# Block 1 loaded in two transfers, a root from ScalarE, LoRA four at a time, and a token sum in two parts: the start of a gated feed-forward kernel

## The chip, the cores and the metric

One core of a Trainium2 chip runs the program. A core has TensorE (PE; its weight loads are shown as PEld), VectorE (DVE), ScalarE (ACT), GpSimd (POOL) and SyncE (SP), which issues most of the DMAs. The metric is the device time of one execution in microseconds (us); before the change it is 442.54 us, the median of 3 runs (442.51 to 442.62).

## The reference

The input x is 2 x 1024 x 512 in f32, so 2048 tokens of 512 values.

```
xn = (x - mean) / sqrt(var + 1e-5)                  # over the 512 values of a token
s  = convolution of xn[token] with a kernel K of length 512, + D * xn
h1 = xn @ w1.T + 2 * (xn @ A1.T) @ B1.T             # 512 -> 1376, LoRA of rank 16
h3 = xn @ w3.T + 2 * (xn @ A3.T) @ B3.T
f  = (silu(h1) * h3) @ w2.T + 2 * (... @ A2.T) @ B2.T
out = x + s * silu(f)
```

The kernel merges each LoRA product into the weight it belongs to. K comes from the parameters of a state-space model; that part lies late in the program and the change doesn't touch it.

## The kernel before, in words

All matmuls are in f32, and TensorE makes two passes of each. The products with w1 and w3 use a fast matrix multiplication of Winograd's kind at two levels: seven products in place of eight, twice. Its operands are sums of quarters of the tokens and of the weights. They are called here T1 to T4 (sums of tokens) and sums of weights; "outer" sums are of the first level and "inner" ones of the second. VectorE makes nearly all of them.

**Tokens.** They stand in four blocks of 512, each of four tiles of 128 tokens. For a block, `load_x` (L225) requests the tiles, `norm_stats` (L244) takes mean and variance of each on VectorE (L247, L248), `norm_root` (L278) makes 1/sqrt(var + eps) by an integer guess and two corrections (`rsqrt`, L50, eight steps, behind one that adds eps and ahead of one that makes the shift), `normalize` (L288) applies it, tiles 0 and 2 on ScalarE (L293) and tiles 1 and 3 on GpSimd (L297), and `transpose` (L299) turns a tile by TensorE (four matmuls with the identity, L304) into a bank of PSUM, from which ScalarE copies it into `xr` (L312, or L314 and L315 for odd blocks). Blocks 0 and 1 make the first pair (sb 0), 2 and 3 the second. Block 3's statistics are made by ScalarE (L254, L265), and one `norm_root` serves blocks 2 and 3. `outer_token_sum` (L317, operations at L328) makes T1 to T4 of a pair in `xt`; `inner_token_sum` (L335) makes the inner sums, T3 at L341, T2 = T3 + b11 at L343, T4 at L345, T1 at L347, each in a raw part over the three rows of `xr` and a second part over the four rows of `xt`. Their results lie in `t_in[7]`, `t_in[6]` and `t_in[4]`; the last two are also where blocks 3 and 2 are loaded.

**Weights.** The hidden 1376 columns are five pairs of 2 x 128 and a last chunk of 96. `load_pair` (L396) fetches a pair's w1 and w3 in four transfers, `load_last` (L463) the last chunk in two. A LoRA product (`lora_product`, L381, matmul at L383) has a contraction of only 16 rows; the factors lie in four groups of 16 rows, at partitions 0, 32, 64 and 96: `lo_d` holds A1 or A3, `lo_h` a part of B1 or B3. Groups 0 and 2 hold the w1 factors, 1 and 3 the w3 factors. `merge_pair` (L408) uses groups 0 and 1 and does one half of a pair; `merge_whole_pair` (L419) uses all four groups for a whole pair at once. The products go into PSUM banks and VectorE adds them to the weights (`merge`, L392, operation at L393).

**Banks.** PSUM has eight banks, two each of the tags x, y, w and aux; `bank(tag)` takes them in turn, and with `borrow` it takes the next one without moving the turn.

**Order.** Each engine runs its instructions in the order in which the program records them, and the order is written out by hand: `at(place, what)` puts a step into a heap, and the heap is emptied in order of place (49 units of place are one pair's seven chains). `after(delay, what)` places a step behind the one now running. A `Chain` (L766 and on) is one product of the second level in seven steps, whose matmuls are all at L756, with copies by ScalarE at L776 and L794 and totals by VectorE at L780. The code ahead of the heap (L965 to L1020) is recorded first, in order: loads, 36 passes on the identity that keep TensorE busy (`keep_warm`), the last chunk's LoRA product, block 0's statistics, root and normalization, four more keep-warm matmuls, block 0's transposes, and then block 1's statistics and root with the merges of the last chunk (L484) between them. The last chunk's product with the first token pair (`last_chain`) is the first real product.

**DMA.** SP and ACT have a queue each. Eight DMA semaphores go round over all transfers of both: a transfer waits, on the engine that issues it, until the eighth before it has landed.

In the built program the first transfers stand so on the two queues:

```
SP : x tiles 0, 2 | lo_d, lo_h group 0 | block 1, four tiles | last w1, w3 | pair 0 (4) |
     blocks 2, 3 (8 tiles) | pair 1 (4) | lo_d, lo_h group 2 | lo_d, lo_h group 3
ACT: x tiles 1, 3 | lo_d, lo_h group 1 | table load
```

Of the kernel before, what the change touches and what calls it, by code (L numbers as in the profile page):

```python
# [12 lines left out]
F32 = mybir.dt.float32  # L13
I32 = mybir.dt.int32
AF = mybir.ActivationFunctionType
# [34 lines left out]
def rsqrt(nc, pool, v, shape):  # L50


    y = pool.tile(shape, F32, tag="rs_y", name="rs_y")
    t = pool.tile(shape, F32, tag="rs_t", name="rs_t")
    part = 3.0 / 8.0
    c2 = part * 0.703952253
    nc.vector.tensor_scalar(
        y.bitcast(I32), v.bitcast(I32), -0.5, float(0x5F1FFFF9), ALU.mult, ALU.add
    )
    nc.vector.tensor_tensor(t, y, y, ALU.mult)  # L60
    nc.vector.scalar_tensor_tensor(t, t, -c2, v, ALU.mult, ALU.mult)
    nc.vector.scalar_tensor_tensor(y, t, c2 * 2.38924456, y, ALU.add, ALU.mult)
    nc.vector.tensor_tensor(t, y, y, ALU.mult)
    nc.vector.scalar_tensor_tensor(t, t, 1.0 / part**2, v, ALU.mult, ALU.mult)
    nc.vector.scalar_tensor_tensor(t, t, -10.0 / 3.0, t, ALU.add, ALU.mult)
    nc.vector.scalar_tensor_tensor(y, t, 5.0, y, ALU.add, ALU.mult)
    return y
# [40 lines left out]
def s4_gated_ffn(  # L108
# [59 lines left out]
    def bank(tag, borrow=False):  # L168

        i = turn[tag]  # L170
        if not borrow:
            turn[tag] = 1 - i
        return psum.tile([P, 512], F32, tag=f"{tag}{i}", name=tag, bufs=1)
# [36 lines left out]
    def value(tag="s"):  # L210
        return upool.tile([P, TB], F32, tag=tag, name=tag, bufs={"s": 10, "c": 4}[tag])
# [7 lines left out]
    def after(delay, what):  # L219
        at(now[0] + delay, what)  # L220
# [2 lines left out]


    def load_x(b):  # L225
        room = (None, None, t_in[4], t_in[6])[b]
        tiles = []
        for tt in range(NTT):
            t = value() if room is None else room[:, tt, :]
            queue = nc.scalar if b == 0 and tt % 2 else nc.sync  # L230
            queue.dma_start(out=t, in_=x[bass.ds(b * TB + tt * P, P), :])
            tiles.append(t)
        return tiles

    norms, sums_of_x = {}, {}

# [38 lines left out]
            norms[b][:, :, 1], sums_of_x[b][:, 2, :], 1.0 / DIM, None, mult  # L275
        )

    def norm_root(mv, *blocks):  # L278
        n = len(blocks) * NTT
        veps = small.tile([P, n], F32, tag="veps", name="veps")  # L280
        nc.vector.tensor_scalar(veps, mv[:, :, 1], EPS, None, add)
        rstd = rsqrt(nc, small, veps, [P, n])
        shift = small.tile([P, n], F32, tag="shift", name="shift")
        nc.vector.scalar_tensor_tensor(shift, mv[:, :, 0], -1.0, rstd, mult, mult)
        for n, b in enumerate(blocks):
            norms[b] = [t[:, n * NTT : (n + 1) * NTT] for t in (rstd, shift)]
# [9 lines left out]
            else:  # L296
                nc.gpsimd.tensor_scalar(t, t, rstd[:, one], shift[:, one], mult, add)  # L297

    def transpose(b, tiles, tag="aux"):  # L299
        sb, low = divmod(b, 2)  # L300
        for tt in tiles:
            ps = bank(tag)
            for dc in range(NDC):
                nc.tensor.transpose(  # L304
                    ps[:, dc * P : (dc + 1) * P],
                    x_in[b][tt][:, dc * P : (dc + 1) * P],
                    ident,
                )
            at_ = slice(tt * P, (tt + 1) * P)
            halves = ps.rearrange("p (c k t) -> p c k t", c=2, k=2)  # L310
            if low == 0:
                nc.scalar.copy(xr[:, 0:2, sb, :, at_], halves)  # L312
            else:
                nc.scalar.copy(b12[sb][:, :, at_], halves[:, 0])  # L314
                nc.scalar.copy(xr[:, 2, sb, :, at_], halves[:, 1])  # L315
# [18 lines left out]

    def inner_token_sum(name, raw, half=None):  # L335
        src, lo, n = (xr, 0, 3) if raw else (xt, 3, 4)
        some = slice(n) if half is None else slice(2 * half, 2 * half + 2)
        to = {i: t[:, lo : lo + n, :][:, some] for i, t in t_in.items()}
        b11, b21, b12_, b22 = (src[:, some, s, k, :] for s in range(2) for k in range(2))
        if name == 3:  # L340
            nc.vector.tensor_tensor(to[7], b22, b12_, sub)  # L341
        elif name == 2:
            nc.vector.tensor_tensor(to[6], to[7], b11, add)  # L343
        elif name == 4:
            nc.vector.tensor_tensor(to[4], b21, to[6], sub)  # L345
        else:
            nc.vector.tensor_tensor(b12_, b12_, b11, sub)  # L347
# [21 lines left out]
    def load_lora(queue, group, d, h, lo, hi):  # L369
        rows = slice(32 * group, 32 * group + R)  # L370
        if d is not None:
            queue.dma_start(out=lora["d"][rows, :], in_=d)
        queue.dma_start(out=lora["h"][rows, : hi - lo], in_=h[:, lo:hi])
        lora["base"][group] = lo
# [6 lines left out]
    def lora_product(ps, group, dc, lo, n, start=True):  # L381
        d, h = lora_factors(group, lo, n)
        nc.tensor.matmul(  # L383
            ps,
            lhsT=d[:, dc * P : (dc + 1) * P],
            rhs=h,
            start=start,
            stop=True,
            skip_group_check=True,
        )  # L390

    def merge(to, ps):  # L392
        nc.vector.scalar_tensor_tensor(to, ps, LORA_SCALE, to, mult, add)  # L393
# [11 lines left out]
                )  # L405
        return w

    def merge_pair(c, w, half, tag="aux"):  # L408

        ps = [bank(tag), bank(tag)]  # L410
        for k in range(2):
            for v in range(2):
                n = slice(k * 2 * P, (k + 1) * 2 * P)
                lora_product(ps[v][:, n], v, 2 * half + k, PAIR_AT[c], 2 * P, k == 0)
        for v in range(2):
            to = w[:, (1, 2, 0, 3)[2 * v + half]].rearrange("p k m h -> p (k m h)")
            after(1.6 + v, lambda to=to, v=v: merge(to, ps[v]))

    def merge_whole_pair(c, w, first=None, delays=(1.15, 2.3, 4.3, 4.4)):  # L419

        ps = [first or [bank("y", True), bank("w", True)], [bank("aux"), bank("aux")]]
# [41 lines left out]
    def load_last():  # L463
        both = const.tile([P, 2, 2 * NDC * LASTR], F32, tag="w2b", name="last")
        w, s = (
            both[:, i].rearrange("p (a b h) -> p a b h", a=n, h=LASTR)
            for i, n in enumerate((2, 4))
        )
        for v, src in enumerate((w1T, w3T)):
            nc.sync.dma_start(  # L470
                out=w[:, v], in_=src[:, LAST * P :].rearrange("(dc p) h -> p dc h", p=P)
            )
        return w, s

    def lora_last():
        ps = [bank("y"), bank("y")]
# [485 lines left out]
        for i, p in places:  # L962
            at(7 * n + p, lambda i=i: step(i))

    x_in = {0: load_x(0)}  # L965
    warm = const.tile([P, 1], F32, name="warm")
    nc.gpsimd.memset(warm, 0.0)
    make_identity(nc, ident)
    lora_tiles(LSPLIT)
    factors = (a1, b1T), (a3, b3T)  # L970
    for v, f in enumerate(factors):
        load_lora((nc.sync, nc.scalar)[v], v, *f, LSPLIT, HID)
    nc.scalar.activation(warm, warm, AF.Silu)
    x_in[1] = load_x(1)
    make_upper_triangular(nc, tri, 1.0, diag=True)
    w_last, s_last = load_last()
    w_pair, s_pair = {0: load_pair(0)}, {c: {} for c in range(NPAIR)}
    x_in[2], x_in[3] = load_x(2), load_x(3)
    w_pair[1] = load_pair(1)
    for v, f in enumerate(factors):  # L980
        load_lora(nc.sync, 2 + v, *f, LSPLIT, HID)

    def other_factors():
        for v, (_, h) in enumerate(factors):
# [18 lines left out]
    ps_last = lora_last()  # L1003
    mv = norm_tile(0)
    norm_stats(0, range(NTT))
    norm_root(mv, 0)
    normalize(0)

    keep_warm(primed[1], 4)
    transpose(0, range(NTT))  # L1010
    mv = norm_tile(1)
    norm_stats(1, range(2))
    merge_last(w_last, ps_last, 0)
    norm_stats(1, range(2, NTT))
    norm_root(mv, 1)
    merge_last(w_last, ps_last, 1)
    mv_late = norm_tile(2, 3)
    ab_last = last_operands(w_last, s_last)

# [37 lines left out]
            add_chain(2 + 7 * c + n, pair_chain(c, n), places)  # L1057
    at(-10, lambda: normalize(1))
    at(-9.9, lambda: last_sums(w_last, s_last))
    at(-9, lambda: merge_pair(0, w_pair[0], 0))  # L1060
    at(-3.8, lambda: merge_pair(0, w_pair[0], 1))
    for i in range(2):
        at(-6 + i, lambda i=i: transpose(1, range(2 * i, 2 * i + 2), "y"))
    for n, name in enumerate((3, 2, 1)):
        at((-2.3, -1.5, -0.45)[n], lambda name=name: outer_token_sum(0, name))
        at(-0.6 + 0.3 * n, lambda name=name: outer_weight_sums(w_pair[0], (name,)))
    at(0.4, lambda: outer_token_sum(0, 4))
    at(0.8, lambda: outer_weight_sums(w_pair[0], (4,)))
    for tt in range(NTT):
        at(-6 + 0.8 * tt, lambda tt=tt: norm_stats(2, (tt,)))  # L1070
        at(-1.4 + 0.1 * tt, lambda tt=tt: act_sums(3, tt))
        at((-0.3, -0.2, 1.7, 1.8)[tt], lambda tt=tt: act_squares(3, tt))
    at(-0.9, lambda: act_means(3))
    at(1.9, lambda: act_variances(3))
    at(6.9, lambda: norm_root(mv_late, 2, 3))
    at(7.3, lambda: normalize(2))
    at(7.7, lambda: normalize(3, (0,)))
    for n, place in enumerate((12.1, 12.8, 13.7, 14.4)):
        b, i = divmod(n, 2)
        at(place, lambda b=b, i=i: transpose(2 + b, range(2 * i, 2 * i + 2)))  # L1080
# [5 lines left out]
        at(when, lambda name=name: inner_weight_sum(w_pair[0], s_pair[0], name))  # L1086
    for name, raw, when, *half in (
        (3, True, 21.6),
        (2, True, 22.8),
        (3, False, 24.2),  # L1090
        (2, False, 30.2),
        (1, True, 34.4),
        (1, False, 37.5, 0),
        (1, False, 40.3, 1),
        (4, True, 47.6),
        (4, False, 50.2, 0),
        (4, False, 52.3, 1),
    ):
        at(when, lambda of=(name, raw, *half): inner_token_sum(*of))
# [495 lines left out]
```

## Time and profile before

| | us |
|---|---|
| median of 3 runs | 442.54 |
| the profiled execution | 442.84 |
| its span, first to last instruction | 441.0 |
| TensorE busy | 434.3 (98%) |
| VectorE busy | 317.6 (72%) |
| GpSimd busy | 207.9 (47%) |
| ScalarE busy | 144.3 (33%) |
| DMA, mean | 122 GB/s |

The page shows one execution. Busy time of TensorE is modelled: its matmuls overlap, and a matmul that waits a little still looks busy, so the distance from one start to the next is the better measure (0.43 us for a pass over 512 columns, 0.11 us over 128). The chain of waits follows the execution back from its end and tells at each step what released it. A timeline merges neighbours of one kind; "x8" behind a row says how many, and the bracket behind it how long the engine was idle and for whom. Times in timelines count from the start of the span.

### The profile page before, as it was taken

What the parts mean: (1) busy time and instruction counts of PE and PEld (TensorE: products, weight loads), DVE (VectorE), ACT (ScalarE), POOL (GpSimd) and SP (SyncE); (2) the same over time, 40 slices, a digit from 0 to 9 for tenths busy, and PEclk for the clock granted to TensorE, in tenths of its full rate; (3) what the DMA queues carried; (4) which work ended last, traced back from release to release, by engine and by line L of the source; (5) the groups of instructions that cost most, each with busy time, mean ns of one, the idle gap of its engine ahead of it and who ended that gap; (6) DMA issues with size and microseconds to landing.
All of it is one profiled execution on the core that took longest, in us unless ns stands there. A gap on an engine that the chain in (4) does not pass through costs nothing.

```text
span 441.0 us, 5158 instructions
## 1 busy us (share of the span) xinstructions
PE 434.3 (98%) x1704; PEld 269.1 (61%) x1704; DVE 317.6 (72%) x536; ACT 144.3 (33%) x296; POOL 207.9 (47%) x156
## 2 busy tenths in 40 slices
PE   7999999999999999999999999999999999999996
PEld 7645334344444444444443446888898999999996
DVE  5899999954974687469745796979786885653234
ACT  2777242453255324532453242211101212212221
POOL 1416468895689368946894468400000122222221
PEclk9999999999999999999999999999999999999999
DMA  8931304025102500250035526395901832422211
GB/s 242 364 83 44 124 0 149 10 84 159 36 24 80 159 24 25 88 170 25 25 129 206 162 94 214 94 364 189 344 33 71 296 129 95 144 97 95 77 67 48
DMA packets 35467, 53.61 MB, mean 122 GB/s; under 512 B 4689, under 2 KB 21521, under 8 KB 35313
## 3 DMA queue, kind: packets, MB, share of 16 engines
q1 hardware_dynamic: 35088, 52.69, 36.3%
q10 hardware_dynamic: 352, 0.60, 0.4%
q8 instruction: 13, 0.21, 0.2%
q14 instruction: 14, 0.11, 0.1%
HBM read 33.88 MB, written 19.40 MB: 121 GB/s over the span
## 4 chain that ended last, share of the span: by engine, by line
PE 86%; DVE 7%; DMA 2%; ACT 2%; issue 1%; POOL 0%; SPq 0%; DVEq 0%; ACTq 0%; POOLq 0%
PE x L756 43%; PE y L756 22%; PE w L756 11%; PE aux L930 4%; PE w L930 2%; DMA s<-in_x_dram 1%; DVE xt L328 1%; DVE s L453 1%; DVE w L441 1%; DMA w<-in_w1T_dram 1%; PE y L529 1%; PE aux L711 1%; DVE t_in L343 1%; ACT c L254 1%; DVE aux L1310 1%
## 5 line engine op out<-in xcount | busy, mean ns | idle before, releaser
L1313 POOL TENSOR_TENSOR o<-o,xin 128x512 f32<-128x512 f32 (+1 forms) x17 | 23.3, 1369 | 133.0 <-DVE o L1312 133.0
L837 POOL TENSOR_TENSOR s<-c,s 128x512 f32<-128x512 f32 (+1 forms) x44 | 63.2, 1442 | 17.6 <-ACT c L829 12.4
L776 ACT COPY s<-x 128x512 f32<-128x512 f32 (+1 forms) x54 | 31.5, 584 | 84.5 <-PE x L756 84.4
L756 PE MATMUL x<-t_in,s 128*128 128x512 f32 (+1 forms) x148 | 55.4, 501 | 0.0
L870 POOL TENSOR_TENSOR s<-ua_three,s 128x512 f32<-128x512 f32 x20 | 35.9, 1793 | 25.4 <-DVE s L780 25.4
L780 DVE TENSOR_TENSOR s<-s,y 128x512 f32<-128x512 f32 (+1 forms) x54 | 36.0, 679 | 15.7 <-PE y L756 10.6
L756 PEld LDWEIGHTS x<-t_in,s 128*128 128x128 f32 x148 | 26.6, 190 | 23.3 <-issue 11.7
L870 POOL TENSOR_TENSOR ua_three<-ua_three,s 128x512 f32<-128x512 f32 x20 | 30.6, 1529 | 13.8 <-DVE s L780 13.8
L756 PE MATMUL y<-t_in,s 128*128 128x256 f32 (+1 forms) x108 | 35.9, 459 | 0.1
L1335 ACT COPY z<-x 128x256 f32<-128x256 f32 x24 | 8.8, 371 | 70.5 <-PE x L756 70.4
L870 POOL TENSOR_TENSOR s<-u_three,s 128x512 f32<-128x512 f32 x20 | 29.4, 1474 | 1.8 <-ACT c L829 1.0
L1310 DVE TENSOR_TENSOR aux<-aux,m 128x384 f32<-128x384 f32 x32 | 18.1, 565 | 15.8 <-PE aux L930 14.3
L829 ACT ACTIVATE c<-c 128x512 f32<-128x512 f32 x40 | 25.2, 632 | 12.9 <-DVE c L870 12.9
L756 PEld LDWEIGHTS y<-t_in,s 128*128 128x128 f32 x108 | 20.1, 190 | 11.6 <-issue 8.1
L794 ACT COPY w<-x 128x512 f32<-128x512 f32 (+1 forms) x37 | 21.1, 570 | 11.6 <-PE x L756 11.5
L870 POOL TENSOR_TENSOR u_three<-ua_three,u_three 128x512 f32<-128x512 f32 x10 | 15.6, 1556 | 13.4 <-DVE u_three L780 13.3
L756 PE MATMUL x<-t_in,w 128*128 128x512 f32 x40 | 21.0, 605 | 0.0
L756 PE MATMUL x<-xt,w 128*128 128x512 f32 x40 | 20.7, 598 | 0.0
L756 PE MATMUL x<-xr,w 128*128 128x512 f32 x40 | 20.6, 614 | 0.0
L756 PE MATMUL x<-xr,s 128*128 128x512 f32 x40 | 20.5, 614 | 0.0
L756 PE MATMUL x<-xt,s 128*128 128x512 f32 x40 | 20.4, 592 | 0.0
L756 PE MATMUL y<-xt,w 128*128 128x512 f32 x40 | 19.8, 592 | 0.0
(302 smaller groups left out, 908.7 us busy)
## 6 DMA issues: line engine op xcount, KB each, us to landing
g_dram<-s SPq DMA_DIRECT2D x40, 256.0 KB, 2.1
g<-g_dram SPq DMA_DIRECT2D x10, 512.0 KB, 5.8
xin<-in_x_dram SPq DMA_DIRECT2D x16, 256.0 KB, 2.7
out_dram<-o SPq DMA_DIRECT2D x14, 256.0 KB, 2.0
t_in<-g_dram SPq DMA_DIRECT2D x6, 512.0 KB, 4.1
w<-in_w1T_dram SPq DMA_DIRECT2D x10, 256.0 KB, 3.6
w<-in_w3T_dram SPq DMA_DIRECT2D x10, 256.0 KB, 4.9
t_in<-in_x_dram SPq DMA_DIRECT2D x8, 256.0 KB, 5.7
```

Source lines behind the costliest of these rows:

```text
L254: nc.scalar.activation(value("c"), x_in[b][tt], AF.Copy, accum_out=sums_of_x[b][:, 0, tt : tt + 1])
L756: nc.tensor.matmul(ps[:, cols], lhsT=lhsT, rhs=rhs if parts == 1 else rhs[:, cols], start=first and i == 0 and part == 0, stop=i == len(pa ...
L776: nc.scalar.copy(t, self.x)
L780: nc.vector.tensor_tensor(t, t, self.y, add)
L794: nc.scalar.copy(self.w, self.x)
L829: nc.scalar.activation(c, c if src is None else src, AF.Silu)
L837: nc.gpsimd.tensor_tensor(g, act, g, mult)
L870: (nc.vector if o < 20 else nc.gpsimd).tensor_tensor(to, a, b, add)
L930: nc.tensor.matmul(to[:, n * P : (n + 1) * P], lhsT=x_, rhs=by, start=start, stop=True, skip_group_check=True,)
L1310: nc.vector.tensor_tensor(y[:, P:], y[:, P:], m[:, n * P : (n + 3) * P], add)
L1313: (nc.vector if last else nc.gpsimd).tensor_tensor(o, o, self.xin[h][:, cols], add)
L1335: nc.scalar.copy(t, xb)
```

## The change

**Loads.** Block 1 goes into `t_in[7]`, in two transfers of 512 KB (tiles 0 and 1 on SP's queue, 2 and 3 on ACT's), requested right behind block 0 and ahead of the LoRA factors. Blocks 2 and 3 come in two transfers each. The LoRA factors of groups 2 and 3 come behind the last chunk and ahead of pair 0.

```
SP : x tiles 0, 2 | block 1, tiles 0-1 | lo_d, lo_h group 0 | last w1, w3 | lo_d, lo_h group 2 |
     lo_d, lo_h group 3 | pair 0 (4) | blocks 2, 3 (2 + 2) | pair 1 (4)
ACT: x tiles 1, 3 | block 1, tiles 2-3 | lo_d, lo_h group 1 | table load (Sqrt)
```

**Root.** Block 0's root starts from ScalarE's Sqrt; VectorE takes the reciprocal and corrects it once (`refined`). ScalarE's first table is Sqrt's, and a second load, with one activation of Silu, stands behind its four copies of block 0.

**LoRA.** Pair 0's product is made whole, from four groups, into the banks y, y, aux, aux, in place of two halves. Its four merges stand behind block 1's root.

**Order.** Three keep-warm matmuls in place of four. Block 0's third tile and block 1's first go through a bank of tag x. The last chunk's second merge stands ahead of block 1's root. Three of block 2's four statistics stand behind the outer sums of the first pair. `normalize(2)` moves behind a copy of ScalarE. The Silu of the last chain's first product stands behind all of block 1's copies. T2's third raw row is made apart, just ahead of T2's second part.

The diff, without the lines that only carry these through:

```diff
     def load_x(b):
+        if b == 0:
+            tiles = [value() for _ in range(NTT)]
+            for tt, t in enumerate(tiles):
+                (nc.sync, nc.scalar)[tt % 2].dma_start(out=t, in_=x[bass.ds(tt * P, P), :])
+            return tiles
+        room = (None, t_in[7], t_in[4], t_in[6])[b]
+        for tt in range(0, NTT, 2):
+            queue = nc.scalar if b == 1 and tt else nc.sync
+            queue.dma_start(
+                out=room[:, tt : tt + 2, :],
+                in_=x[bass.ds(b * TB + tt * P, 2 * P), :].rearrange("(n p) d -> p n d", p=P),
+            )
+        return [room[:, tt, :] for tt in range(NTT)]
+    def refined(mv, veps):
+        ...
+        nc.scalar.activation(root, mv[:, :, 1], AF.Sqrt, bias=eps)
+        nc.vector.tensor_scalar(veps, mv[:, :, 1], EPS, None, add)
+        nc.vector.reciprocal(y, root)
+        nc.vector.tensor_tensor(t, y, y, mult)
+        nc.vector.scalar_tensor_tensor(t, t, -0.5, veps, mult, mult)
+        nc.vector.scalar_tensor_tensor(y, t, 1.5, y, add, mult)
+        return y
     def inner_token_sum(name, raw, half=None):
-        some = slice(n) if half is None else slice(2 * half, 2 * half + 2)
+        some = slice(n) if half is None else slice(2 * half, min(2 * half + 2, n))
-    x_in = {0: load_x(0)}
+    x_in = {0: load_x(0), 1: load_x(1)}
-    nc.scalar.activation(warm, warm, AF.Silu)
-    x_in[1] = load_x(1)
+    nc.scalar.activation(warm, warm, AF.Sqrt)
+    w_last, s_last, load_of_last = load_last()
+    for v in range(2):
+        load_of_last(v)
+    for v, f in enumerate(factors):
+        load_lora(nc.sync, 2 + v, *f, LSPLIT, HID)
     w_pair, s_pair = {0: load_pair(0)}, {c: {} for c in range(NPAIR)}
     x_in[2], x_in[3] = load_x(2), load_x(3)
     w_pair[1] = load_pair(1)
-    for v, f in enumerate(factors):
-        load_lora(nc.sync, 2 + v, *f, LSPLIT, HID)
-    norm_root(mv, 0)
+    norm_root(mv, 0, on_act=True)
-    keep_warm(primed[1], 4)
-    transpose(0, range(NTT))
+    keep_warm(primed[1], 3)
+    for tt, tag in enumerate(("aux", "aux", "x", "aux")):
+        transpose(0, (tt,), tag)
+    nc.scalar.activation(warm, warm, AF.Silu)
     norm_stats(1, range(2, NTT))
+    merge_last(w_last, ps_last, 1)
     norm_root(mv, 1)
-    merge_last(w_last, ps_last, 1)
-    at(-9, lambda: merge_pair(0, w_pair[0], 0))
-    at(-3.8, lambda: merge_pair(0, w_pair[0], 1))
-    for i in range(2):
-        at(-6 + i, lambda i=i: transpose(1, range(2 * i, 2 * i + 2), "y"))
+    at(
+        -9,
+        lambda: merge_whole_pair(
+            0, w_pair[0], [bank("y"), bank("y")], (1.6, 1.7, 1.8, 1.9)
+        ),
+    )
+    at(-6, lambda: transpose(1, (0,), "x", True))
+    at(-5.9, lambda: transpose(1, range(1, NTT), "y"))
-        at(-6 + 0.8 * tt, lambda tt=tt: norm_stats(2, (tt,)))
+        at((-6, 0.84, 0.85, 0.9)[tt], lambda tt=tt: norm_stats(2, (tt,)))
-    at(7.3, lambda: normalize(2))
-    at(7.7, lambda: normalize(3, (0,)))
+    at(7.7, lambda: normalize(2))
+    at(7.75, lambda: normalize(3, (0,)))
-        (2, True, 22.8),
+        (2, True, 22.8, 0),
         (3, False, 24.2),
+        (2, True, 30.1, 1),
         (2, False, 30.2),
```

More of the change, by code (lines that the diff above doesn't have):

```diff
@@ L225, in load_x @@
     def load_x(b):
[L226 to L233, printed above, removed]
+        if b == 0:
[11 more added lines that the diff above has]
+        return [room[:, tt, :] for tt in range(NTT)]
     norms, sums_of_x = {}, {}
@@ L276, in act_variances, with norm_root @@
         )
-    def norm_root(mv, *blocks):
+    def refined(mv, veps):
+        shape = list(veps.shape)
+        y = small.tile(shape, F32, tag="rs_y", name="rs_y")
+        t = small.tile(shape, F32, tag="rs_t", name="rs_t")
+        root = small.tile(shape, F32, tag="root", name="root", bufs=1)
+        nc.scalar.activation(root, mv[:, :, 1], AF.Sqrt, bias=eps)
[5 more added lines that the diff above has]
+        return y
+    def norm_root(mv, *blocks, on_act=False):
         n = len(blocks) * NTT
         veps = small.tile([P, n], F32, tag="veps", name="veps")
-        nc.vector.tensor_scalar(veps, mv[:, :, 1], EPS, None, add)
-        rstd = rsqrt(nc, small, veps, [P, n])
+        if on_act:
+            rstd = refined(mv, veps)
+        else:
+            nc.vector.tensor_scalar(veps, mv[:, :, 1], EPS, None, add)
+            rstd = rsqrt(nc, small, veps, [P, n])
         shift = small.tile([P, n], F32, tag="shift", name="shift")
@@ L297, in normalize, with transpose @@
                 nc.gpsimd.tensor_scalar(t, t, rstd[:, one], shift[:, one], mult, add)
-    def transpose(b, tiles, tag="aux"):
+    def transpose(b, tiles, tag="aux", borrow=False):
         sb, low = divmod(b, 2)
         for tt in tiles:
-            ps = bank(tag)
+            ps = bank(tag, borrow)
             for dc in range(NDC):
@@ L406, in load_pair @@
         return w
[L408 to L417, printed above, removed]
     def merge_whole_pair(c, w, first=None, delays=(1.15, 2.3, 4.3, 4.4)):
@@ L468, in load_last, with load @@
         )
-        for v, src in enumerate((w1T, w3T)):
+        def load(v):
             nc.sync.dma_start(
-                out=w[:, v], in_=src[:, LAST * P :].rearrange("(dc p) h -> p dc h", p=P)
+                out=w[:, v],
+                in_=(w1T, w3T)[v][:, LAST * P :].rearrange("(dc p) h -> p dc h", p=P),
             )
-        return w, s
+        return w, s, load
     def lora_last():
@@ L963, in add_chain @@
             at(7 * n + p, lambda i=i: step(i))
-    x_in = {0: load_x(0)}
+    x_in = {0: load_x(0), 1: load_x(1)}
     warm = const.tile([P, 1], F32, name="warm")
-    nc.gpsimd.memset(warm, 0.0)
+    eps = const.tile([P, 1], F32, name="eps")
+    for t, v in ((warm, 0.0), (eps, EPS)):
+        nc.gpsimd.memset(t, v)
     make_identity(nc, ident)
@@ L972, in s4_gated_ffn @@
         load_lora((nc.sync, nc.scalar)[v], v, *f, LSPLIT, HID)
-    nc.scalar.activation(warm, warm, AF.Silu)
-    x_in[1] = load_x(1)
+    nc.scalar.activation(warm, warm, AF.Sqrt)
+    w_last, s_last, load_of_last = load_last()
+    for v in range(2):
+        load_of_last(v)
     make_upper_triangular(nc, tri, 1.0, diag=True)
-    w_last, s_last = load_last()
+    for v, f in enumerate(factors):
+        load_lora(nc.sync, 2 + v, *f, LSPLIT, HID)
     w_pair, s_pair = {0: load_pair(0)}, {c: {} for c in range(NPAIR)}
```

## The prediction, made before the changed kernel was run

> **What bounds the kernel now.** The page's first two parts come first: one engine fills the span.
>
> ```profile
> PE 434.3 (98%) x1704; PEld 269.1 (61%) x1704; DVE 317.6 (72%) x536; ACT 144.3 (33%) x296; POOL 207.9 (47%) x156
> PE   7999999999999999999999999999999999999996
> DVE  5899999954974687469745796979786885653234
> ```
>
> TensorE is busy 98% of the span. The change takes almost no work from it, so its worth lies in the first 60 us: how early TensorE's stream runs dense, and whether VectorE feeds it from there on. So the second view is the busy time by stage:
>
> ```profile
> 2.20:4.80 2.60, 2.60 (x14) 2.60 (x14) 0.78 (x2) 1.49 (x2) 0.00 (x0) 1.00 1.01 381
> 5.00:7.00 2.00, 2.00 (x16) 2.00 (x16) 1.22 (x3) 0.00 (x0) 0.00 (x0) 1.00 1.03 132
> 20.90:61.70 40.80, 40.73 (x137) 17.61 (x135) 39.33 (x58) 22.91 (x53) 16.76 (x12) 1.00 0.25 78
> ```
>
> The columns are stretch, length, busy time of PE, PEld, DVE, ACT and POOL, clock, DMA share and GB/s. From 20.9 to 61.7 us VectorE is busy 39.33 of 40.80 us: it is as full as TensorE. At 5 to 7 us the DMA engines are fully busy but move 132 GB/s instead of 381; the first four LoRA transfers (lo_d and lo_h, 16 rows each, 140 KB in all) are landing then. The third view is the chain of waits from 20 to 63 us, and the fourth the timelines of VectorE and TensorE at its end:
>
> ```profile
> 45.60 2.41 DVE xt L328 x4
> 48.01 0.60 DVE s L780
> 48.61 2.40 DVE xt L328 x4
> 51.01 1.68 DVE t_in L341
> ...
> 52.79 2.64 DVE t_in L343
> ...
> 57.27 1.96 PE x L756 x4
> ```
>
> ```profile
> 59.34 2.27 DVE L343 TENSOR_TENSOR t_in<-t_in,xt 128x2048 f32<-128x2048 f32 x1
> ```
>
> ```profile
> 61.67 1.12 PE L756 MATMUL x<-t_in,s 128*128 128x512 f32 x2
> ```
>
> The chain runs on VectorE. T2's second part (L343) ends at 59.34 + 2.27 = 61.61, and the matmul that reads it starts at 61.67. There is no slack at that point: whatever VectorE is later there, TensorE is later. The last view is the head:
>
> ```profile
> 7.89 1.28 PE L383 MATMUL y<-lo_h,lo_d 16*128 16x96 f32 x16
> 9.10 1.16 PE L991 MATMUL w<-ident 128*128 128x128 f32 x8
> 11.01 1.09 PE L304 MATMUL aux<-ident,s 128*128 128x128 f32 x8 [0.75 <-ACT s L293]
> 21.55 1.29 DVE L328 TENSOR_TENSOR xt<-xr,b 128x512 f32<-128x512 f32 x2 [0.64 <-ACT xr L315]
> ```
>
> ```profile
> lo_h<-in_b3T_dram ACTq DMA_DIRECT2D x1, 38.0 KB, 5.8
> ```
>
> TensorE does the last chunk's LoRA product at 7.89, when the last of the four transfers has landed (issued 2.11, 5.8 us later: 7.9), then keeps warm, then transposes block 0 at 11.01. Block 1's transposes and evictions let VectorE begin the outer sums at 21.55.
>
> **Part by part.**
>
> *Block 0's statistics and root.* Tiles 2 and 3 wait 0.74 us for their load at 6.43. With nothing but block 1 behind them in the queues they should land near 5, as the first two (3.98) at 381 GB/s, so the sums end 0.74 earlier: 8.17 becomes 7.43. The root took from 8.17 to 10.14, ten steps of 0.20. Now ScalarE's Sqrt (0.20, the row of the warm-up activation, and two hand-overs of 0.03) and five VectorE steps of 0.20 (the 128x4 reciprocal has a row of 178 ns): 1.26. Normalizing starts at 8.7 instead of 10.14, the first tile is ready at 9.6 instead of 11.0. ScalarE's first table load slips behind an issue that waits for the second tile (4.14): it ends near 6.1, hidden by the sums.
>
> *The LoRA transfers behind block 1.* Rings are served in order of issue (landings in the trace follow it), and 1.05 MB now stand ahead of lo_d and lo_h: 2.75 us at 381 GB/s. Block 0's data end at about 4.75, block 1's at 7.5. Lower end of the landing L: 0.37 us for 140 KB and 0.3 until it is seen: 8.2. Upper end: 7.94 + 2.75 = 10.7, the slow stretch repeated. It is the row of the same transfers, so I stay near it, but the 264 KB of the stretch from 5 to 7 us were half other data (block 1's first tiles), which now lie ahead: of the 3.2 us from 4.75 to 7.94 I keep 2.4. L = 9.9.
>
> TensorE executes in order. From the last landing to the keep-warm matmuls it took 1.16 (7.94 to 9.10), and six passes instead of eight take 0.77: transposes can start at L + 1.93 = 11.83. The normalized tiles, ready at 9.6, wait. Only below L = 7.7 would the faster root count.
>
> *From the transposes to the outer sums.* Before: 11.01 to 21.55, 10.54 us. The third tile in bank x takes ScalarE's gap between evictions away: 3.16 to the last eviction becomes 2.77, -0.39. The four-at-a-time LoRA of pair 0 takes the place of the first half: 1.07 (the 16 passes from 30.48 to 31.55) for 1.05, so nothing on this path; the second half (21.47 to 22.53) goes. The Silu that stood between block 1's evictions moves behind them: the third tile's eviction comes 0.5 earlier, the fourth, which waits for a bank, 0.17. ScalarE's second table load with its activation, 1.28 + 0.20, and the copy of 0.56 come to 2.04; beside it TensorE does the chain's second half and the LoRA, 0.97 + 1.07 = 2.04. The cover is just enough. VectorE's statistics of block 1 wait inside for the last chunk's merge, and its root ends near 15.8 as before (15.78). Block 1's tiles on ScalarE follow the table load and are ready before TensorE comes to them at 18.6. Sum: 9.98. The outer sums start at 11.83 + 9.98 = 21.8 (+0.26).
>
> [...]
>
> *VectorE from 21.55 to 61.62*, 40.07 us. Two merges of pair 0 have moved ahead of it (pitch 0.60 each): -1.20. Three of block 2's four statistics have moved into it, 0.79 each by their pitch at 18.45 and 19.24: +2.38. In before they filled the wait up to 21.55, so there they cost nothing. ScalarE's copy ahead of normalize(2) takes away a wait of 0.24 (34.20), later statistics one of 0.11 (30.17). T2's third raw row apart adds about 0.05; it brings the first raw rows forward by 0.57 (a third of 1.74), but T2's second part follows the third row, so its end doesn't move. Together +0.88. T2's second part ends at 61.62 + 0.26 + 0.88 = 62.76.
>
> *TensorE* loses 1.05 of LoRA, but then waits for the first outer sum: 21.81 + 0.79 = 22.6 against 22.53. It gets to the matmul of 61.67 at 61.7 and waits until 62.8. Behind it VectorE's next operand was there 2.6 us early (62.62 for about 65.2), so the delay passes on whole. **Sum: L - 8.76 = +1.1 us.** The profiled execution is 442.84 us (span 441.0 and 1.8 around it), 0.30 over the median of 442.54. 442.84 + 1.1 gives 443.9 for it, and 443.7 for a median.
>
> The other queues: SP's four LoRA loads of groups 2 and 3 go ahead of pair 0's weights, which land 1 to 1.5 us later (15.6 becomes about 17). The merges that read them run behind the root and end near 19.4, ahead of 21.8: hidden by 2 us. Blocks 2 and 3 land where they did.
>
> **The rivals.**
>
> *Not slower: the loads land right behind block 1.* Speaks for it: eight engines' packets of lo_h took 98 ns before the slow stretch. L = 8.2 to 8.8 gives -0.56 to 0.04, some 442.2. It decides from L = 9.65 down: there the sum is 0.89, or 0.2%. Against it: 132 GB/s in the row, and lone 16-row loads at 32.5 us whose packets took 120 to 390 ns.
>
> *Faster: VectorE's stalls fall away.* Three operations of the stretch took longer than their equals while GpSimd held one: L453 2.19 for 1.09, L441 1.65 for 0.68, L343 2.64 for 1.74, in all 2.97. Shifted by half a microsecond, two of them may miss: 1.14 - 1.97 = -0.8 at L = 9.9; with L = 8.2 it is -2.5, but TensorE's own arrival (0.07 at L = 9.9, so -1.6) then ends last. Some 441.3.
>
> *Slower by more.* One stall of 1 us is added, or the table load's cover fails (up to 1.28 more), or TensorE, idle from 7.6 to L, falls back to the slow pace that it shows until 5.80 (213 ns a pass, then 111): some 15 passes more at 0.1 and slower chain steps, 1.5. About 445.0. [...]
>
> **How the numbers follow.** 0.2% (0.89 us) is about what a measurement of this kernel can tell from no change. The forecast (L 9.3 to 10.7, stalls as before: 443.1 to 444.5) 0.50, of it 0.37 over 443.43 and 0.13 within; loads early 0.18, within; stalls gone 0.22, faster; more slow 0.10. So faster 0.22, same 0.31, slower 0.47. For the range, L's ends with a stall more or less give 441.0 to 445.5; cut to 8 in 10: 441.2 to 445.1. The likeliest case alone: 443.1 to 444.5.
>
> **What would show it.** Right: the first LoRA product starts near 10 and transposes near 11.8 though block 0 is normalized by 9.6; outer sums near 21.8; TensorE idle about 1 us ahead of the first matmul on T2's second part. Wrong: the product before 9; outer sums before 20.5; that matmul without a wait.

## The result: slower by 1.1%, and the profile after

The changed kernel takes **446.89 us** in the median of 4 runs (445.31 to 449.72); the kernel before took 442.52 beside it. The ratio is 1.0111, with a 95% interval of 1.0086 to 1.0136. Forecast were 443.7 us and a range of 441.2 to 445.1: the direction was right, the size was not, and the time lies above the range. The profiled execution took 446.47 us (span 444.7, 3.7 more than before's 441.0).

In the changed kernel L405 is before's L383 (LoRA product), L1008 L991 (keep-warm), L326 L304 (transposes), L350 L328 (outer sums), L365 L343 (T2) and L770 L756 (chains).

From the page, busy time, the rows of TensorE and VectorE and the granted clock, with the clock row of the kernel before under them:

```profile
PE 433.8 (98%) x1702; PEld 269.3 (61%) x1702; DVE 316.2 (71%) x533; ACT 146.0 (33%) x299; POOL 208.6 (47%) x157
PE   5999999999999999999999999999999999999996
DVE  5689999973975497448845796979786885653234
PEclk9899999999999999999999999999999999999999
```

```profile
PEclk9999999999999999999999999999999999999999
```

TensorE's busy time is even a little smaller than before; the 3.7 us are no work. They lie in the first slices: the first of TensorE is 5 in place of 7, and the clock row has an 8 in its second slice, where before's had 9 throughout. The busy time by stage (stretch, length, PE, PEld, DVE, ACT, POOL, clock, DMA share, GB/s) shows what that is:

```profile
2.20:4.80 2.60, 2.60 (x14) 2.60 (x14) 0.71 (x2) 0.22 (x1) 0.00 (x0) 1.00 1.00 375
5.00:7.00 2.00, 2.00 (x20) 2.00 (x19) 1.93 (x5) 1.07 (x2) 0.00 (x0) 1.00 1.02 358
7.40:10.60 3.20, 0.20 (x2) 0.20 (x2) 2.52 (x10) 1.81 (x3) 1.52 (x2) 1.00 1.24 190
11.70:14.80 3.10, 3.10 (x15) 3.10 (x15) 2.93 (x10) 0.56 (x1) 0.00 (x0) 0.50 0.93 257
23.30:65.40 42.10, 40.38 (x128) 16.88 (x126) 40.83 (x62) 23.26 (x53) 19.29 (x13) 1.00 0.21 70
```

The slow stretch of the DMA engines has moved from 5 to 7 us (132 GB/s before) to 7.4 to 10.6 us (190 GB/s). TensorE is idle in nearly all of it, and from 11.7 to 14.8 us it runs 15 passes at a granted clock of 0.50. The last of the first four LoRA transfers was issued at 4.23 and landed at 10.59 (2.11 and 7.94 before):

```profile
lo_h<-in_b3T_dram ACTq DMA_DIRECT2D x1, 38.0 KB, 6.4
```

TensorE's timeline of that time:

```profile
1.77 5.51 PE L1008 MATMUL w<-ident 128*128 128x128 f32 x35
10.40 1.38 PE L405 MATMUL y<-lo_h,lo_d 16*128 16x96 f32 x16 [3.11 <-DMA lo_h<-in_b1T_dram]
11.71 1.65 PE L1008 MATMUL w<-ident 128*128 128x128 f32 x6
13.14 1.91 PE L326 MATMUL aux<-ident,s 128*128 128x128 f32 x8
14.85 0.69 PE L326 MATMUL x<-ident,s 128*128 128x128 f32 x4
```

Eight transposes took 1.09 before and take 1.91 here; the four behind them, from 14.85, take 0.69, with the granted clock back at 1.00 from 15.03. At the other end of the head, the timelines of VectorE and of TensorE:

```profile
23.90 1.29 DVE L350 TENSOR_TENSOR xt<-xr,b 128x512 f32<-128x512 f32 x2 [1.69 <-ACT xr L337]
...
62.60 2.76 DVE L365 TENSOR_TENSOR t_in<-t_in,xt 128x2048 f32<-128x2048 f32 x1
```

```profile
65.42 1.12 PE L770 MATMUL x<-t_in,s 128*128 128x512 f32 x2 [0.73 <-DVE t_in L365]
```

The outer sums start 2.35 us later than before, T2's second part ends at 65.36 (61.62), and its first matmul starts at 65.42 (61.67): 3.75 later, which the span then keeps (3.7). The chain of waits stays on VectorE here to the end of the stretch. In before it left VectorE behind the operation at 55.42 and ran over TensorE from 57.27: there the two were tied at T2's second part (no wait at 61.67), here TensorE waits 0.73 us for it:

```profile
58.68 2.20 DVE t_in L363
...
62.68 2.68 DVE t_in L365
65.36 2.08 DVE s L464
```

### The profile page after: what moved, and what is told of

It reads as the page before. It is cut to its first block, busy times and chain, and to the rows that moved or that the text cites. A ratio compares the mean times of both kernels' runs of the same rounds, so it can differ in the third digit from the quotient of the medians.

```text
span 444.7 us, 5156 instructions
## 1 busy us (share of the span) xinstructions
PE 433.8 (98%) x1702; PEld 269.3 (61%) x1702; DVE 316.2 (71%) x533; ACT 146.0 (33%) x299; POOL 208.6 (47%) x157
## 4 chain that ended last, share of the span: by engine, by line
PE 83%; DVE 4%; issue 1%; ACT 0%; DVEq 0%
PE x L770 42%; PE y L770 21%; PE w L770 11%; PE aux L944 4%; PE w L944 2%; DVE t_in L363 1%; DVE t_in L365 1%; PE y L405 1%; PE y L543 1%; PE aux L725 1%; DVE aux L1334 0%; DVE s L464 0%; DVE xt L350 0%; DVE o L1336 0%; PE aux L655 0%
## 5 line engine op out<-in xcount | busy, mean ns | idle before, releaser
L851 POOL TENSOR_TENSOR s<-c,s 128x512 f32<-128x512 f32 (+1 forms) x44 | 66.9, 1526 | 13.6 <-ACT c L843 11.1
L770 PE MATMUL x<-t_in,s 128*128 128x512 f32 (+1 forms) x148 | 55.5, 502 | 0.9 <-DVE t_in L365 0.7
L794 DVE TENSOR_TENSOR s<-s,y 128x512 f32<-128x512 f32 (+1 forms) x54 | 36.0, 678 | 15.7 <-PE y L770 10.6
L884 POOL TENSOR_TENSOR s<-ua_three,s 128x512 f32<-128x512 f32 x20 | 32.6, 1632 | 26.3 <-DVE s L794 26.3
L770 PEld LDWEIGHTS x<-t_in,s 128*128 128x128 f32 x148 | 26.5, 190 | 24.5 <-issue 11.5
L770 PE MATMUL y<-t_in,s 128*128 128x256 f32 (+1 forms) x108 | 35.8, 458 | 0.0
L884 POOL TENSOR_TENSOR ua_three<-ua_three,s 128x512 f32<-128x512 f32 x20 | 29.6, 1481 | 12.6 <-DVE s L794 12.6
L770 PEld LDWEIGHTS y<-t_in,s 128*128 128x128 f32 x108 | 20.2, 190 | 11.1 <-issue 8.6
L770 PE MATMUL x<-t_in,w 128*128 128x512 f32 x40 | 20.9, 603 | 0.0
L770 PE MATMUL x<-xr,w 128*128 128x512 f32 x40 | 20.6, 614 | 0.1
L770 PE MATMUL x<-xt,w 128*128 128x512 f32 x40 | 20.6, 597 | 0.0
L770 PE MATMUL x<-xr,s 128*128 128x512 f32 x40 | 20.5, 613 | 0.0
L770 PE MATMUL x<-xt,s 128*128 128x512 f32 x40 | 20.4, 592 | 0.0
L770 PE MATMUL y<-xt,w 128*128 128x512 f32 x40 | 19.8, 592 | 0.0
```

The lines of the kernel that those rows point to most:

```text
L770: nc.tensor.matmul(ps[:, cols], lhsT=lhsT, rhs=rhs if parts == 1 else rhs[:, cols], start=first and i == 0 and part == 0, stop=i == len(pa ...
L794: nc.vector.tensor_tensor(t, t, self.y, add)
L851: nc.gpsimd.tensor_tensor(g, act, g, mult)
L884: (nc.vector if o < 20 else nc.gpsimd).tensor_tensor(to, a, b, add)
```

## The experiments

The theory after the two traces: the loss starts with the order of the loads. The LoRA transfers land late, TensorE's fixed order makes it wait for them, the pause lets its pace fall back, and VectorE's longer stretch comes on top. The rivals: the second table load, VectorE alone, or the pause without the pace.

All edits are to the changed kernel unless another is named; times are medians, with the range in brackets.

| | us | ratio to before (95%) | granted clocks |
|---|---|---|---|
| e1 LoRA loads first | 444.14 (442.3-445.93) | 1.0037 (1.0021-1.0053) | 0.996-1.000 |
| e2 transposes first | 449.53 (445.39-451.01) | 1.0149 (1.0114-1.0183) | 0.987-0.999 |
| e3 pause filled | 446.15 (445.13-446.7) | 1.0079 (1.0062-1.0095) | 0.998-1.000 |
| e4 statistics early | 447.1 (446.4-448.13) | 1.0103 (1.0085-1.0121) | 0.991-0.994 |
| e5 before, order alone | 447.11 (444.06-449.4) | 1.0092 (1.0058-1.0126) | 0.990-1.000 |
| e6 e1 + statistics early | 446.35 (444.82-449.93) | 1.0091 (1.0063-1.012) | 0.990-0.998 |
| e7 changed kernel again | 447.81 (445.69-448.8) | 1.0111 (1.0091-1.0132) | 0.992-0.999 |
| e8 e2, pauses filled | 446.27 (445.99-446.55) | 1.008 (1.0067-1.0093) | 0.998-1.000 |
| e9 e1, means on ScalarE | 443.48 (442.67-443.83) | 1.0021 (1.0012-1.0029) | 0.998-1.000 |
| e10 e6, means on ScalarE | 441.92 (441.5-443.09) | 0.9994 (0.9985-1.0002) | 0.998-1.000 |
| e11 before, root alone | 441.93 (441.19-442.2) | 0.9989 (0.998-0.9997) | 0.998-1.000 |
| e12 e3 + e10's mends | 445.36 (444.03-446.63) | 1.0071 (1.0052-1.009) | 0.998-1.000 |

**e1: the order undone.**

```diff
-    x_in = {0: load_x(0), 1: load_x(1)}
+    x_in = {0: load_x(0)}
...
         load_lora((nc.sync, nc.scalar)[v], v, *f, LSPLIT, HID)
+    x_in[1] = load_x(1)
```

> The changed kernel with one thing undone: the first four LoRA transfers stand ahead of block 1 again. My theory (the late LoRA landing starts the loss): they land near 7.9 in place of 10.6, TensorE's pause ends near 8, the transposes start near 9.8 (13.1 in the changed kernel, now held by the first normalized tile at 9.6), the outer sums near 20.3, and 3.4 to 3.7 us are gained: 442.8 to 443.6 us. Rival, the second table load or VectorE's longer stretch carries the loss: less than 1 us is gained, 446 or more. Second rival, block 1 then lands so late (near 11) that its root takes the place of the transposes: 444.5.

Its trace (442.3 us) is as expected: the LoRA transfers land at 7.29, the transposes start at 9.69, the outer sums at 19.73. Timelines of TensorE and VectorE:

```profile
7.66 1.13 PE L405 MATMUL y<-lo_h,lo_d 16*128 16x96 f32 x16
8.73 0.94 PE L1009 MATMUL w<-ident 128*128 128x128 f32 x6
9.69 1.09 PE L326 MATMUL aux<-ident,s 128*128 128x128 f32 x8
```

```profile
19.73 1.29 DVE L350 TENSOR_TENSOR xt<-xr,b 128x512 f32<-128x512 f32 x2 [1.29 <-ACT xr L337]
```

No pause, and no wait of the transposes. The median, 444.14, gains 2.75 on 446.89 (3.07 when each is taken against the kernel before that ran beside it), less than the 3.4 expected, and its runs reach from 442.3 to 445.9. Most of the loss is the order; something else strikes some runs (e9).

**e2: TensorE doesn't wait for the LoRA transfers.** `lora_last()` is recorded behind block 0's transposes, and the merges of the last chunk behind block 1's root.

```diff
-    ps_last = lora_last()
...
         transpose(0, (tt,), tag)
+    ps_last = lora_last()
...
     norm_root(mv, 1)
+    merge_last(w_last, ps_last, 0)
+    merge_last(w_last, ps_last, 1)
```

> The changed kernel, loads as they are, but TensorE does block 0's transposes ahead of the last chunk's LoRA product, and the two merges of that product stand behind block 1's root. My theory (TensorE's fixed order makes it wait for the LoRA transfers): the transposes start near 9.7 at the fast pace, the LoRA product near 11.7 without a wait, the last chain's first step near 15.0 (15.8), outer sums near 21.6 (23.9), 444.5 us. Rival, the landing itself is what matters whatever stands behind it: the last chain is as late as before and the time stays at 446.9.

The one trace is near it (transposes 9.66, LoRA product 11.64 without a wait, 445.39 us), but TensorE waits for the merges instead, 1.75 us (the releaser named was over by then; the first merge, behind the root on VectorE, ended at 14.42):

```profile
14.52 1.94 PE L770 MATMUL x<-xr,last 128*96 128x256 f32 x8 [1.75 <-ACT warm L1029]
```

The median is 449.53, the worst of all, with clocks down to 0.987. In its trace TensorE transposes 3.48 us earlier than in the changed kernel (9.66 for 13.14) and pauses twice (1.09 and 1.75 us); the median is 2.64 us slower. That called for e8.

**e3: the pause filled.** `keep_warm(ps, 9, True)` becomes `keep_warm(ps, 16, True)`.

> The changed kernel with 32 primed passes in place of 18, so that TensorE is busy until shortly before the LoRA transfers land. Theory that the pause costs by the pace after it: landings as before (10.6), but the six keep-warm passes take 0.7 in place of 1.43 and all transposes go at 0.11 a pass; transposes start near 12.5, outer sums near 22.7, 445.4 to 445.8 us, and the times scatter less than 445.3 to 449.7. Rival, the pace doesn't reach the end: VectorE's work decides, 446.9 as before.

446.15, with clocks of 0.998 and more, and the scatter falls from 4.4 to 1.6 us. In its trace the transfers land at 11.35, later than in the changed kernel, and yet the transposes start at 13.22, nearly the same: six keep-warm passes take 0.77 in place of 1.43. So the pace is a term of its own. The gain in the median, 0.7, is below the 1.1 to 1.5 expected. Two things stay open here. In both traces with 32 primed passes (e3, and e12 with 11.47) the landing is later than in the five that have 18 and the same order of loads (10.38 to 11.12). And e3's two runs at a clock of 1.000 took 446.62 and 446.70, the changed kernel's one 445.31: the filling may have a price of its own, which no run isolates.

**e4: VectorE's statistics back.**

```diff
-        at((-6, 0.84, 0.85, 0.9)[tt], lambda tt=tt: norm_stats(2, (tt,)))
+        at(-6 + 0.8 * tt, lambda tt=tt: norm_stats(2, (tt,)))
```

> The changed kernel with block 2's three statistics back in their earlier places, ahead of the outer sums. Theory that VectorE's longer stretch is a term of its own: VectorE is 2.4 us less loaded behind the outer sums, TensorE's wait ahead of T2's second part (0.9) and the smaller ones before it (about 1.0 together) go, 445.2 to 446.0 us. Rival, all of the loss comes from the head: 446.9 as before. Second rival, the statistics wait for block 2 (20.1) and push the outer sums later: 447.5.

The time didn't move (447.1): taken alone the expectation failed. The trace says why: the transfers landed at 11.12, TensorE paused 3.90 us and then ran to 17.9 at half pace (1.91 us for eight transposes, 1.09 in before); all five runs have clocks of 0.994 or less. On VectorE the effect is there: from the outer sums' start to T2's end 39.58 us (26.61 to 66.19) against 41.46, and TensorE waits 0.20 there in place of 0.73. The head hid it; e10 shows it in a time.

**e5: before, with the order alone.** `x_in[1] = load_x(1)` moves up to `load_x(0)`, its four tiles alternating between the queues.

> The kernel before with one thing changed: block 1's four tiles are requested right behind block 0's and ahead of the first four LoRA transfers, alternately on the two queues. Theory (the order of the loads is enough for the loss): the LoRA transfers land near 10.6, TensorE starts the last chunk's product there after a pause of 3 us, the transposes start near 13 (11.0 before), and T2's second part follows 2 us later; with the pace falling back in most runs 444.5 to 446.5 us, and clocks under 0.998 in some runs. Rival, the loss needs the other parts (second table load, LoRA at once, later statistics): 443 us or less.

447.11 us, above the 444.5 to 446.5 expected and 4.4 over the kernel before, so the order alone is enough for the whole loss. The LoRA transfers land at 10.94. Waits of TensorE and its timeline:

```profile
PE y L383 <- DMA lo_h<-in_b1T_dram: 2.3, 1, 2.3
```

```profile
10.84 2.22 PE L383 MATMUL y<-lo_h,lo_d 16*128 16x96 f32 x16 [2.27 <-DMA lo_h<-in_b1T_dram]
12.99 2.08 PE L990 MATMUL w<-ident 128*128 128x128 f32 x8
14.86 3.41 PE L304 MATMUL aux<-ident,s 128*128 128x128 f32 x16
```

A pause of 2.27 us, and behind it a granted clock of 0.50 from 10.98 to 17.75 us (the stretch stands further down). Of its six runs the two with clock 1.000 took 444.06 and 444.49, the one with 0.990 took 449.4.

**e6: e1 with two of the late statistics early.** e1, and `(-6, -5.2, -4.4, 0.9)[tt]` as the places of `norm_stats(2, ...)`.

> The changed kernel with the LoRA transfers ahead of block 1 again (as in e1) and two of block 2's three late statistics back ahead of the outer sums, where VectorE waited 1.3 us in e1. Theory of two terms: the outer sums start 0.2 later than in e1 (20.0), VectorE ends T2's second part 1.3 earlier (59.9 in place of 61.2), TensorE's wait of 0.89 ahead of it goes; 441.0 us for an execution like e1's profiled one (442.3), 442.8 for the median (444.1). Rival, e1's loss against its profiled execution comes from the same place on VectorE: then the median gains more than 1.3. Second rival, VectorE isn't the limit in e1: 444.1 again.

All three answers were wrong: 446.35, slower than e1. GpSimd's timeline of e6 and of e1, and TensorE's of e6:

```profile
23.99 4.07 POOL L265 TENSOR_SCALAR act_sums<-act_sums 128x4 f32<-128x4 f32 x1 [4.10 <-ACT c L259]
28.03 0.22 POOL L266 TENSOR_SCALAR mv<-act_sums 128x4 f32<-128x4 f32 x1
```

```profile
23.24 0.28 POOL L265 TENSOR_SCALAR act_sums<-act_sums 128x4 f32<-128x4 f32 x1 [4.08 <-ACT c L259]
```

```profile
30.22 1.93 PE L770 MATMUL x<-xt,last 128*96 128x512 f32 x4 [2.50 <-ACT s L790]
```

The same small operation, four numbers a partition, takes 0.28 us in e1 and 4.07 in e6. VectorE ran `TENSOR_TENSOR` operations without a gap from 20.70 to 27.98; when the last ended and a `BATCH_NORM_STATS2` ran, GpSimd's ended too (28.06). ScalarE's squares of block 3 wait for it, ahead of a copy that TensorE waits for: 2.5 us. In this execution the granted clock stayed at 1.00 from 4.70 to 36.00 us, over the wait; the five other runs of e6 have clocks of 0.990 to 0.996.

**e7: the changed kernel again.**

> The changed kernel as it is, for a second trace and more times. If the pause decides the scatter, a time is about 445 us plus what the granted clock lost, which is (1 - clock) x span: 445 at 1.000, 446.8 at 0.996, 449.5 at 0.990; median 446 to 447. Rival, the scatter comes from elsewhere: the times don't go with the clock.

447.81, above the 446 to 447 expected. The times go with the clock. Time, clock, and time less (1 - clock) x span:

| changed kernel | us | clock | less what the clock lost |
|---|---|---|---|
| first four runs | 445.31, 446.47, 447.31, 449.72 | 1.000, 0.996, 0.996, 0.990 | 445.3, 444.7, 445.5, 445.2 |
| e7 | 445.69, 447.0, 447.13, 448.49, 448.7, 448.8 | 0.999, 0.996, 0.996, 0.992, 0.992, 0.992 | 445.2, 445.2, 445.3, 444.9, 445.1, 445.2 |

All ten come to 445.1 within 0.4, though they lie 4.4 us apart. Its trace has the same picture (landing 11.01, pause 3.20, clock 0.996). By the same subtraction e4's runs come to 443.3 to 444.1, under all ten of these, which fits a gain on VectorE that the pace hid.

The subtraction is good only for the large losses. The mean clock also counts a slow stretch at the end of the program: in the trace of before the only one after the start begins at 439.29 us, behind TensorE's last matmul (it ends at 437.25). Of the 29 runs of before beside e9 to e12, the eight at 0.998 took 442.25 in the mean and the thirteen at 1.000 took 442.48. So 0.998 or 0.999 is no sign of a loss.

**e8: e2 with its pauses filled.** `keep_warm(primed[1], 3)` becomes 8, and `keep_warm(primed[1], 8)` follows the LoRA product.

> e2 (transposes ahead of the LoRA product; 449.5 us in the median, 445.4 in its profiled execution) with both of TensorE's pauses filled by passes on the identity: ten more ahead of the transposes, sixteen behind the LoRA product. Theory that the pauses make the pace fall back in most of e2's runs: clocks of 0.998 and more, 444.5 to 446 in all runs. Rival, e2's loss in the timed runs comes from later loads and not from the pace: 449 again.

446.27, all five runs within 0.6 us, clocks of 0.998 and more: 3.3 faster than e2 by passes that compute nothing. The median lies 0.3 over the expected range; the rival (449) is out. Not all of the 3.3 is shown to be pace: with the clock taken off, e2's six runs still lie between 444.9 and 447.4. Against the changed kernel, e8 is only 0.6 us faster.

**e9: e1 without GpSimd's three small operations.**

```diff
-        nc.gpsimd.tensor_scalar(sums[:, 1, :], sums[:, 0, :], -1.0 / DIM, None, mult)
+        nc.scalar.activation(sums[:, 1, :], sums[:, 0, :], AF.Copy, scale=-1.0 / DIM)
```

and likewise the mean and the variance.

> e1 with block 3's means and variances (three operations of 128x4) on ScalarE in place of GpSimd. Theory: in e6's trace one of these GpSimd operations took 4.07 us in place of 0.28 while VectorE ran one operation after another, TensorE waited 2.5 us and its pace fell back; the same may strike some runs of e1, whose times reach from 442.3 to 445.9. Without GpSimd there: 442 to 443.2 in nearly all runs, median 442.6, clocks of 0.998 and more. Rival, e1's scatter comes from the landing of the loads: 444.1 again and as wide.

443.48, 0.9 over the expectation, but the scatter goes: 442.67 to 443.83, where e1 has 442.3 to 445.93. That fits a GpSimd operation as long as e6's (4.07 us) in some of e1's runs; in e1's only trace it takes 0.28, so for e1 it isn't shown.

**e10: e6 in the same way.**

> e6 (LoRA transfers first, two of three late statistics early) with the same three operations on ScalarE. Theory: the wait of 2.5 us at 27 goes, T2's second part starts near 60 in place of 61.2 as in e1, 441.0 to 441.7 us, clocks of 0.998 and more: faster than both kernels. Rival, the statistics ahead of the outer sums cost what they gain: 442.5 or more.

441.92: 4.4 faster than e6, and 1.56 faster than e9, from which it differs only in two statistics. T2's second part begins at 57.78 (e9 59.37). It lies 0.2 over the range expected, and against before the interval includes 1, so it isn't shown to be faster.

**e11: before, with the root alone.** `norm_root(mv, 0, on_act=True)` with `refined`, the Sqrt table first and the Silu load behind block 0's copies.

> The kernel before with only block 0's root from ScalarE's Sqrt (and the second table load, with one activation, behind the four copies of block 0). By the trace of before: TensorE is ready for the transposes at 10.26 and waited until 11.01 for a normalized tile, so they start 0.75 earlier, and VectorE, which sets the end, too: 441.9 us. Rival, the second table load isn't covered (1.3 us ahead of a copy that TensorE waits for): 442.5 to 443.5.

441.93, as expected, and the only version here that is shown to beat both kernels (the one before by 0.03 to 0.2%). The transposes start 0.55 earlier and wait for nothing:

```profile
10.46 1.04 PE L321 MATMUL aux<-ident,s 128*128 128x128 f32 x8
```

**e12: the order kept, the rest mended.** 32 primed passes, e6's places, e9's ScalarE operations.

> The changed kernel with its order of loads kept and the rest mended: 32 primed passes (as in e3), two of the late statistics early, the three small operations on ScalarE. Theory: e3's 446.15 less about 1.3 for VectorE: 444.8 us, and the difference to e10 (3 to 3.5) is what the order of the loads costs by itself. Rival, the order costs nothing once the pause is filled: within 1 us of e10.

445.36, 0.6 over the expectation. It differs from e10 in the order of the loads and in the filled pause, and costs 3.44 more: the order has its price also where the pause is filled (with the filling's own price, if it has one, inside).

## Why the prediction was wrong in size

The sum was L - 8.76, with L the landing of the LoRA transfers. Its shape held; the profiled execution shows where 2.6 us were missing at the end of T2's second part (65.36 for 62.76):

| step | predicted | measured | missing |
|---|---|---|---|
| L | 9.9 | 10.59 | 0.69 |
| L to the transposes | 1.93 | 2.55 | 0.62 |
| transposes to outer sums | 9.98 | 10.76 | 0.78 |
| outer sums to T2's end | 40.95 | 41.46 | 0.51 |

*Statistics and root:* right. Normalizing starts at 8.78 (8.7), and e11 gives the root's own gain.

*L:* the upper end of the range was the truth (10.59, 11.01, 11.12 in three traces with this head; 10.7 was the end, and two of the three lie beyond it). The step that failed is the 2.4 us that I kept of the slow 3.2, because half of the data in it "now lie ahead". The 16-row transfers run beside block 1's second transfer: 7.4 to 10.6 us moved 190 GB/s (375 from 2.2 to 4.8), and block 1 itself landed at 9.67, where I had 7.5. The 0.3 us until a landing is seen, in the lower end, was my estimate and isn't shown. The premise that landings follow the order of issue failed too: SP's first lo_d, issued behind both halves of block 1, landed at 9.10, ahead of ACT's half.

*The pace:* the step that failed most. The fall-back after the pause was named, priced at 1.5 us, and given a tenth with the table load and a stall. It came in eight of the ten runs of e7's table: 0.62 + 0.78 = 1.40 us in this execution, and up to 4.4 us between runs. Where the pause is missing, e1 has 10.04 from the transposes to the outer sums and e3 has 9.93, with 1.87 from the landing to the transposes, so the 9.98 and the 1.93 were sound for a dense TensorE. The pace is not the whole miss: the run at a clock of 1.000 took 445.31, still over the range; the rows of L and VectorE (0.69 and 0.51 on a forecast of 443.7) come near it. The price was an estimate from the slow passes at the start of before (213 ns each): TensorE's longest wait in before, behind its first matmul, is 0.75 us, so no row there shows what follows a longer one. Here it paused 3.11 us (up to 10.40) and the granted clock was 0.50 from 11.61 to 15.03; in e5 it paused 2.27 us (up to 10.84) and the clock was 0.50 from 10.98 to 17.75. Stretches of e5 and of e6:

```profile
10.98:17.75 6.77, 6.77 (x37) 6.18 (x38) 4.21 (x16) 1.18 (x3) 0.73 (x1) 0.50 1.00 322
```

```profile
4.70:36.00 31.30, 26.60 (x148) 15.66 (x147) 25.76 (x71) 21.28 (x47) 11.83 (x14) 1.00 0.70 214
```

e6's pause, 2.50 us (27.72 to 30.22), is longer than e5's, and the clock stayed at 1.00. So in these traces the length of a pause alone doesn't decide whether the pace falls back. What does, and why the slow pace lasts 3.4 us here and about 7 in e4 and e5, is open.

*VectorE:* 41.45 to 41.46 in four traces with late statistics (e1, e3 and both of the changed kernel; 41.53 in e9), where 40.95 was forecast. 0.49 of the 0.51 is T2's second part itself, 2.76 us for 2.27: one more stall, while a GpSimd operation (L851, 3.20 us from 63.28) runs beside it. With two statistics early it is 39.92 (e10): 1.6 less, as two pitches of 0.79.

*The table load:* right. ScalarE's timeline of e1, where the head is dense, and TensorE's:

```profile
12.45 1.28 ACT L1030 ACT_TABLE_LOAD   x1
13.74 0.20 ACT L1030 ACTIVATE warm<-warm 128x1 f32<-128x1 f32 x1
```

```profile
14.66 1.96 PE L770 MATMUL w<-xr,last 128*96 128x512 f32 x4
```

TensorE's LoRA passes end at 14.65 and the next chain step starts at 14.66: the cover is just enough.

*The rivals:* "not slower" needed L under 9.65, which no trace of this order has. VectorE's stalls moved but didn't shrink: the excess of the slow operations over their equals is about 3.1 us in before's stretch and about 3.6 in this one. (The prediction's 1.97 for two of its three stalls is about two thirds of their 2.97; no two of its rows give it.) "Slower by more" was the case, and beyond its 445.0: by the cause that I had priced at 1.5 us and given a tenth with two others, together with a second of the three, a stall (0.49), and with L.

## What to carry to other kernels

Ask of each transfer that is moved back which engine stands still for it in program order, and price the pause with what follows it: here TensorE waited 3.11 us, and then ran 15 passes at a granted clock of 0.50 (0.62 + 0.78 us on the way to the outer sums). If the wait can't be removed, passes that compute nothing can be worth it (3.3 us from e2 to e8, but only 0.7 from the changed kernel to e3). And where a path is tied between two engines, work moved from a gap into the tied stretch costs its full length (1.56 us for two statistics), however small the engine's busy share is.

## What the runs showed of the hardware

A GpSimd operation on 128x4 took 0.28 us in e1's trace and 4.07 us in e6's (23.99 to 28.06). In e6 VectorE ran `TENSOR_TENSOR` operations back to back beside it: six of them began and ended while it stood, and it ended within 0.1 us of the last one (27.98). Why it stood so long isn't shown. That its place on GpSimd costs time, e10 shows: with the three operations on ScalarE the median is 4.4 us lower. In e1, with the same operations around it, it took its 0.28 us; what decides that is open.

The slow pace after a pause shows in a run's mean granted clock: a clock of 0.990 over 445 us is 4.4 us lost, and the ten runs of the changed kernel, 4.4 us apart, agree within 0.8 us once it is taken off (e7). A clock of 0.998 showed no loss: eight runs of before at 0.998 took 442.25 us in the mean, thirteen at 1.000 took 442.48, and the one slow stretch after the start in before's trace begins at 439.29 us, behind TensorE's last matmul.
